# A gated GNN followed by a GCN on one core: the adjacency turned by VectorE in 4-byte words, and the last TensorE transposes of activations replaced by exchanges

## The chip, the core and the metric

The kernel runs on one core of a Trainium2 chip. Five engines take their instructions from queues of their own: TensorE (PE, with its weight loads shown apart as PEld), VectorE (DVE), ScalarE (ACT), GpSimd (POOL), and SyncE (SP), which here only issues DMA transfers. The metric is the device time in microseconds (us) of one execution. A measured time is the median of several runs; the profile is of one more execution, with its own time.

## The reference, cut to what matters

Sixteen graphs of 1024 nodes with 128 features each; `adj` is a 0/1 matrix of 1024 x 1024 for every graph.

```
h = relu(layernorm(x))
for i in range(4):                          # gated GNN, every graph by itself
    hw = h @ weight[i]
    m  = adj^T @ hw                         # einsum 'bjn,bjd->bnd'
    r  = sigmoid(m @ w_ih.T + h @ w_hh.T ...);  z = sigmoid(...)
    n  = tanh(...);  h = (1 - z) * n + z * h
x = x + h * nodemask
h = relu(layernorm(x))
for i in range(4):                          # GCN
    h = relu(adj @ (h @ W[i]) + b[i])       # einsum 'bnm,bmc->bnc'
    h = gamma[i] * (h - mean) * rsqrt(var + 1e-5) + beta[i]   # mean, var over all graphs and nodes
x = x + h
```

The first network multiplies by the transposed adjacency, which is what a plain load of rows gives to TensorE as moving operand. The second multiplies by the adjacency itself, so the matrix must be turned once for each graph.

## The kernel before

**Two stages.** `exact_path` first runs the gated network over all graphs, and then the GCN layer by layer over all graphs. Between them lie, in DRAM, the turned adjacency in bf16 (`adjT_d`), the sum after the first network (`xmid_d`) and its normalised form (`ymid_d`). A flag (`low`) notes whether the adjacency was exact in bf16; a general path, not run with these inputs, would follow otherwise.

**The gated stage** works on two streams, `sa` (graphs 0, 2, 4 ...) and `sb` (1, 3, 5 ...). A half step (`half_step(one, two)`) does the gates of a layer for stream `two` and, behind it on TensorE, the aggregation of the next layer for stream `one`; then the roles change. Eight half steps take each stream through four layers. On TensorE a half step is 24 gate matmuls (two passes each, L1008) in two halves of 512 nodes and 32 aggregation matmuls (L526: 8 blocks of 128 rows, a high and a low part of the features, two halves of nodes). The features are split in a rounded high part and a remainder (`high`, `low`, L933 and L940) so that TensorE's faster number format loses nothing.

On VectorE a half of a half step is, in the order of its queue: the reset gate (L1027, L1028), `less` (L1044, or L1042 for a stream's first layer), `scaled` (L1048), `low` of the other stream (L940 or L956), `mixed` (L1052), and a transposition of the new features in 32 x 32 blocks (L728). The 32 x 32 blocks are put in their places through DRAM: SP writes them (`exchange_out`, L599) and reads them back in four pieces (`exchange_in`, L606). So most of the turns between features-by-nodes and nodes-by-features need no TensorE.

An order written by hand (`tc.manual_schedule`) fixes all queues in this stage. Other work is entered in an agenda (`at(clock, place, work)`) and taken out at named places of a half step: "start" and "load" before the gates, "beside0/1" within them, "mid" between the halves (GpSimd first waits there for the first half's result, the `pace` copy of L1114), "gap" after both halves. After a graph's last layer, `plan` enters the sum with x and its statistics (`tail_sums`, "gap" two half steps later), the store of that sum, the normalisation, and then the load and statistics of the stream's next graph (`next_sums`, "gap" five half steps later).

**Turning the adjacency.** GpSimd rounds each 128-row block to bf16 (`transpose_rows`, L623), SP issues a DMA transpose of it (L624), and after eight blocks GpSimd issues a store of 2 MB (L637). The generator `transposes` and the class `Feed` spread these over the half steps. There are two bf16 buffers, so a cast waits until an earlier DMA transpose has read its buffer. GpSimd also rounds the loaded rows for the aggregation (L579).

**TensorE transposes that are left** (matmuls by the identity): 8 for x of graph 1 (`turn(sb.y, ...)`, L708; 8 more for graph 0 stay), 8 for the first new features of graph 0 (`split_step`, which is `features_times` with `w is None`, L499), 16 for the last features of graphs 14 and 15 (`last_tail`, L743), and 8 in each of three GCN layers for graph 0 (`raw_split`, L499).

**The GCN stage** is placed by a scheduler. For each graph SP loads eight bf16 blocks of the turned adjacency (L1347), VectorE and ScalarE widen them to the matmul format into 12 row buffers (L1352, L1350), TensorE does 32 aggregation matmuls. In layer 0 `first_split` loads `ymid_d` (into one of four shared buffers) and splits it. In later layers `conv_input` normalises the features of a graph on ScalarE (L1384). The even graphs' blocks use the buffer of tag "adjT" (one), the odd graphs' the eight of tag "half".

**The end.** The last statistics, the normalisation of all 16 graphs (L1548 in halves for graphs 0 and 1, L1542 whole for the others), 128 TensorE transposes (L1554), the sum with x (L1556) and 33 output transfers by SP (L1557).

Of the kernel before, what the change touches and what calls it, by code (L numbers as in the profile page):

```python
# [11 lines left out]
U16 = mybir.dt.uint16  # L12
# [329 lines left out]
def exact_path(  # L342
# [149 lines left out]
    def features_times(w, hT, hw, g, name):  # L492

        pt = tmp(f"hw_{name}_{g}")
        for q in range(BH):
            j = g * BH + q
            src = hT[:, j * P : (j + 1) * P]
            if w is None:
                nc.tensor.transpose(pt[:, q * P : (q + 1) * P], src, ident)  # L499
            else:  # L500
                nc.tensor.matmul(pt[:, q * P : (q + 1) * P], src, w, start=True, stop=True)
        cols = slice(g * HALF, (g + 1) * HALF)
        nc.scalar.copy(hw[0][:, cols], pt)  # L503
        nc.vector.tensor_sub(hw[1][:, cols], pt, hw[0][:, cols].bitcast(F32))
# [30 lines left out]
    with ExitStack() as st:  # L535
# [35 lines left out]

        def stage_rows(b, stage, js):
            for j in js:
                nc.sync.dma_start(stage[j % 4], adj[b][j * P : (j + 1) * P, :])
# [7 lines left out]
        def glance(b, stage, js):  # L582

            junk = work.tile([P, N], BF16, tag="junk", name=f"junk{b}_{js[0]}", bufs=1)
# [5 lines left out]
        def row_sums(rows, js):  # L590

            for j in js:
                junk = work.tile([P, N], BF16, tag="junk", name=f"summed{j}", bufs=1)
                nc.scalar.activation(junk, rows[j].bitcast(F32), AF.Copy, accum_out=by_row[:, j : j + 1])

        def exchange_out(t, name, d=None):
            if d is None:
                d = rawd.tile([P, HALF], F32, tag="cross", name=f"cross_{name}", bufs=8)
            nc.sync.dma_start(d, t)  # L599
# [8 lines left out]
        def pair_in(d, t):  # L608

            src = d.rearrange("h (t r) (s x) -> s r (h t) x", t=4, s=4)  # L610
            for s in range(4):
                nc.sync.dma_start(t[s * 32 : (s + 1) * 32, :].rearrange("r (a x) -> r a x", a=8), src[s])
# [7 lines left out]
        def transpose_rows(b, row, j, adjT):  # L620

            t = work.tile([P, N], BF16, tag="half1", name=f"half{b}_{j}", bufs=2)
            nc.gpsimd.tensor_copy(t, row.bitcast(F32))  # L623
            return lambda: nc.sync.dma_start_transpose(adjT[:, :, j * P : (j + 1) * P], t)  # L624

        def transposes(batches):

            for b, rows in batches:
                adjT = turned_tile(f"adjT{b}")
                ahead = transpose_rows(b, rows[0], 0, adjT)  # L630
                for j in range(NB):
                    go = ahead
                    if j + 1 < NB:
                        ahead = transpose_rows(b, rows[j + 1], j + 1, adjT)
                    go()
                    yield j
                nc.gpsimd.dma_start(adjT_d[b].rearrange("k p n -> p k n"), adjT)  # L637
                yield NB

        class Feed:  # L640


            jobs, full, stored = iter(()), False, False

            def some(self, n):
                for _ in range(n):
                    if not self.full:
                        self.full = next(self.jobs, None) == NB - 1

            def store(self):  # L650
                if self.full and not self.stored:
                    self.stored = next(self.jobs) == NB

            def next_step(self):
                if self.stored:
                    self.full = self.stored = False

        feed, agenda = Feed(), {}
# [68 lines left out]
        def half_out(t, src, hf, name, d=None):  # L727
            turned = nc.vector.transpose(by_nodes(t), four_ways(src[:, hf * HALF : (hf + 1) * HALF]))  # L728
            return exchange_out(t, f"{name}_{hf}", d), turned
# [4 lines left out]
        def tail_sums(b, xt, hT, parts=None):  # L734

            for hf in range(NH):
                if parts:
                    pt = by_nodes(parts[hf])
                else:
                    pt = tmp(f"pt_x{b}_{hf}")  # L740
                    for q in range(BH):
                        k = hf * BH + q
                        nc.tensor.transpose(pt[:, q * P : (q + 1) * P], hT[:, k * P : (k + 1) * P], ident)  # L743
                    pt = four_ways(pt)
                for q in range(BH):
                    k = hf * BH + q
                    xk = xt[:, k, :].rearrange("p (a c) -> p a c", a=4)
                    mask = maskT[:, b * NB + k : b * NB + k + 1]
                    nc.vector.scalar_tensor_tensor(xk, pt[:, q, :, :], mask, xk, ALU.mult, ALU.add)
            return norm_stats(xt, f"mid{b}")  # L750
# [13 lines left out]

        def last_tail(b, xt, hT):
            nt = tail_sums(b, xt, hT)
            y = y_mid(b) if b + 1 < B else xt.rearrange("p k c -> p (k c)")
            store_xmid(b, xt)

            def rest():  # L770
                norm_apply(xt, y, nt)
                store_ymid(b, y)

            return rest
# [3 lines left out]
        class Stream:  # L778
# [54 lines left out]
            def plan(self, n, tail=None):  # L833

                if tail:
                    b, xt, hT, parts = tail
                    end = {}

                    def sums():
                        end["norm"] = tail_sums(b, xt, hT, parts)  # L840
# [11 lines left out]
                    at(n + 5, "mid", lambda: store_ymid(b, end["y"]))  # L852
                if self.b + 2 < B:
# [5 lines left out]
                    at(n + 7, "end", self.ins_away)  # L859

# [44 lines left out]
            def half_away(self, hf):  # L905

                if self.i + 1 - hf == L and self.b + 2 < B:
                    if hf == 0:
                        self.pair = rawd.tile([NH, P, HALF], F32, tag="pair", name=f"pair_out{self.b}", bufs=4)
                    half_out(cross_tile(f"t_out{self.b}_{hf}"), self.new, hf, f"out{self.b}", self.pair[hf])  # L910
# [5 lines left out]
            def halves_back(self):  # L916
                nm = f"{self.b}_{self.i}"
                self.backs = [cross_tile(f"n_h{nm}_{hf}") for hf in range(NH)]
# [25 lines left out]
            def split_step(self):  # L944
                nm = f"{self.b}_{self.i}"
                self.hw = hw_tiles(self.b, f"ghw{nm}")
                for g in range(NH):
                    features_times(None, self.hT, self.hw, g, f"g{nm}")

# [11 lines left out]
            def agg_rows(self, js):  # L961
# [3 lines left out]
                if js[-1] == NB - 1:  # L965
                    self.m = []
                    for hf in range(NH):
                        m = work.tile([P, HALF], F32, tag="m", name=f"m{self.b}_{self.i}_{hf}", bufs=4)
# [22 lines left out]
            def products(self, hf):  # L991
# [28 lines left out]
                self.z = work.tile([P, HALF], F32, tag="z", name=f"z{nm}")  # L1020
# [36 lines left out]
            def finish(self):  # L1057
# [3 lines left out]
                args = self.b, self.xt, self.hT  # L1061
                self.b, self.i = self.b + 2, 0
                if self.b >= B:
                    self.rest = last_tail(*args)
# [3 lines left out]
                parts = [args[-1][:, hf * HALF : (hf + 1) * HALF] for hf in range(NH)]  # L1068

                last = args[-1]  # L1070
                at(clock[0] + 1, "ins", lambda: pair_in(ins, h_in))
                at(clock[0] + 1, "outs", lambda: pair_in(outs, last))
                self.plan(clock[0], (*args, parts))
# [10 lines left out]
        def first_step(one, two, gated, halfway, rest=None):  # L1084

            if one.outs:
                one.halves_back()
                feed.jobs = transposes([(s.b, s.rows) for s in (sa, sb)])
            else:
                one.split_step()  # L1090
            feed.some(2)
            two.gate_step(0)
            two.half_away(0)
            if one.outs:
                for g in range(NH):
                    one.high(g)
                    one.low(g)
            feed.some(2)
            two.gate_step(1)
            two.half_away(1)  # L1100
            gated()
            one.agg_step(0)
# [507 lines left out]
```

## Time and profile before

| what | value |
|---|---|
| median of 3 runs | 1767.48 us (1766.98 to 1768.0) |
| profiled execution, its time | 1767.31 us |
| span of its instructions | 1765.3 us |
| granted TensorE clock, mean | 0.998 |
| DMA, mean over the span | 228 GB/s |
| ACT ended by waits for VectorE's reset gate (L1031) | 151.9 us idle |
| GpSimd idle in front of the bf16 casts (L623), for DMA transposes | 402.7 us |

The span runs from the first to the last instruction; about 2 us of the execution lie around it. In the tables of the profile a group gives the line, the engine, the operation, the tile written and read, the shapes, the count, then the time in which at least one of the group was busy, the mean of one in ns, and the idle time of the engine just ahead of them. In the timeline a row has start, length, engine, line, operation, tiles and, in brackets, the idle time before it with what ended it. Matmuls overlap, so the time per matmul is read from the starts, not from the length of one.

### The profile page before, as it was taken

Reading aid. Unit: us, or ns where it says so; the run is one execution under the profiler, and the core shown is the slowest. Engines: PE = TensorE matmul, PEld = TensorE weight load, DVE = VectorE, ACT = ScalarE, POOL = GpSimd, SP = SyncE. Lnnn points to the kernel's source line nnn. Section 1 sums busy time; section 2 is a strip of 40 time slices with the busy share of each in tenths; the row PEclk is TensorE's granted clock in tenths of the full one; section 3 lists DMA queues with packets and bytes.
Section 4 is the critical chain, followed back from the end, with each engine's and each line's share of the span. In section 5 each row is a group of like instructions: output and inputs, shape, how many; then the busy total and the mean of one; then the engine's idle time right before and its main releaser. Section 6 shows DMA issues by size and latency. Waiting matters only on the chain. (4 is left out here: it accounts for less than half of the span.)

```text
span 1765.3 us, 22293 instructions
## 1 busy us (share of the span) xinstructions
PE 1747.9 (99%) x6710; PEld 1189.1 (67%) x6710; DVE 1289.1 (73%) x2311; ACT 1123.1 (64%) x1729; POOL 374.3 (21%) x404
## 2 busy tenths in 40 slices
PE   9999999999999999999999999999999999999997
PEld 5565656565656565656565656577778888888886
DVE  7686977877877877877787686776666666666665
ACT  5366556557566556655755654486777777767765
POOL 4124323322322332422422323110100000000010
PEclk9999999999999999999999999999999999999999
DMA  7479788677777777778867968888865766757666
GB/s 256 97 195 301 153 217 296 163 208 249 205 200 235 222 188 229 248 183 216 274 158 192 307 150 223 283 310 304 300 219 198 252 224 221 255 202 264 216 235 256
DMA packets 377778, 401.74 MB, mean 228 GB/s; under 512 B 158396, under 2 KB 255456, under 8 KB 377648
## 3 DMA queue, kind: packets, MB, share of 16 engines
q1 hardware_dynamic: 358736, 331.98, 62.9%
q0 software_dynamic: 18384, 67.99, 11.1%
q8 instruction: 55, 0.90, 0.2%
q14 instruction: 75, 0.61, 0.1%
q10 hardware_dynamic: 528, 0.26, 0.0%
HBM read 268.52 MB, written 98.05 MB: 208 GB/s over the span
## 5 line engine op out<-in xcount | busy, mean ns | idle before, releaser
L526 PE MATMUL pm<-row,ghw 128*128 128x512 f32 x2048 | 504.4, 403 | 0.6 <-POOL row L565 0.5
L526 PEld LDWEIGHTS pm<-row,ghw 128*128 128x128 f32 x2048 | 383.6, 188 | 107.7 <-issue 25.5
L526 PE MATMUL pc_m<-wide,chw 128*128 128x512 f32 x1024 | 245.2, 395 | 0.0
L623 POOL CAST half<-row 128x1024 bf16<-128x1024 f32 x128 | 148.6, 1171 | 421.3 <-DMA adjT<-half 402.7
L526 PEld LDWEIGHTS pc_m<-wide,chw 128*128 128x128 f32 x1024 | 190.4, 188 | 41.9 <-issue 3.8
L1031 ACT ACTIVATE r<-r,vecs 128x512 f32<-128x512 f32 x128 | 92.3, 721 | 153.6 <-DVE r L1028 151.9
L526 PE MATMUL pc_g_r<-wide,chw 128*128 128x512 f32 x464 | 186.9, 403 | 0.3 <-ACT chw L503 0.3
L969 ACT COPY m<-pm 128x512 f32<-128x512 f32 x128 | 68.7, 588 | 185.0 <-PE pm L526 185.0
L526 PE MATMUL pc_g_z<-wide,chw 128*128 128x512 f32 x464 | 181.0, 390 | 0.0
L1027 DVE SCALAR_TENSOR_TENSOR r<-g_hn,vecs,r 128x512 f32<-128x512 f32 x128 | 93.2, 728 | 119.4 <-ACT r L1026 68.4
L579 POOL CAST row<-stage 128x1024 fp32r<-128x1024 f32 x112 | 129.1, 1160 | 214.1 <-DMA stage<-in_adj_dram 177.0
L1352 DVE CAST wide<-block 128x1024 fp32r<-128x1024 bf16 x160 | 109.5, 691 | 74.1 <-PE pc_m L526 49.2
L1352 DVE CAST wide<-packed 128x1024 fp32r<-128x1024 bf16 x160 | 110.2, 693 | 70.9 <-PE pc_g_z L526 53.2
L1350 ACT CAST wide<-packed 128x1024 fp32r<-128x1024 bf16 x96 | 100.6, 1047 | 56.4 <-PE pc_m L526 27.6
L1350 ACT CAST wide<-block 128x1024 fp32r<-128x1024 bf16 x96 | 100.4, 1049 | 53.5 <-PE pc_g_z L526 27.7
L1008 PE MATMUL g_r<-m,w_mT 128*128 128x512 f32 x256 | 130.8, 592 | 0.2 <-ACT m L969 0.2
L1008 PE MATMUL g_z<-m,w_mT 128*128 128x512 f32 x256 | 130.7, 592 | 0.0
L1008 PE MATMUL g_xn<-m,w_mT 128*128 128x512 f32 x256 | 130.7, 592 | 0.0
L1048 DVE TENSOR_TENSOR h<-h,z 128x512 f32<-128x512 f32 x128 | 112.6, 880 | 14.4 <-ACT z L1035 2.2
L1026 ACT ACTIVATE r<-g_r,brz 128x512 f32<-128x512 f32 x128 | 87.9, 687 | 48.0 <-PE g_r L1008 47.6
L1400 DVE BATCH_NORM_STATS2 stats<-feat 128x6 f32<-128x512 f32 x128 | 84.1, 685 | 46.6 <-ACT feat L1399 45.6
L1044 DVE TENSOR_TENSOR h<-h,r 128x512 f32<-128x512 f32 x96 | 73.4, 765 | 56.4 <-ACT r L1031 56.4
(186 smaller groups left out, 2817.1 us busy)
## 6 DMA issues: line engine op xcount, KB each, us to landing
block<-adjT_d SPq DMA_DIRECT2D x256, 256.0 KB, 4.7
packed<-adjT_d SPq DMA_DIRECT2D x256, 256.0 KB, 5.7
stage<-in_adj_dram SPq DMA_DIRECT2D x120, 512.0 KB, 5.4
adjT_d<-adjT POOLq DMA_DIRECT2D x16, 2048.0 KB, 8.4
cross_h<-t_h SPq DMA_DIRECT2D x94, 256.0 KB, 2.5
n_h<-cross_h SPq DMA_DIRECT2D x376, 64.0 KB, 2.1
xmid_d<-x POOLq DMA_DIRECT2D x16, 512.0 KB, 7.2
y<-ymid_d POOLq DMA_DIRECT2D x16, 512.0 KB, 6.8
```

The source lines that it names most:

```text
L526: nc.tensor.matmul(pm[hf], hw[s][:, j * P : (j + 1) * P], rows[j][:, hf * HALF : (hf + 1) * HALF], start=(j == 0 and s == 0), stop=(j == N ...
L579: nc.gpsimd.tensor_copy(t, stage[j % 4])
L623: nc.gpsimd.tensor_copy(t, row.bitcast(F32))
L1008: nc.tensor.matmul(po, wT[:, i, g * C : (g + 1) * C], rhs, start=start, stop=stop)
L1026: nc.scalar.activation(r, pr, AF.Sigmoid, bias=brz[:, 3 * i : 3 * i + 1])
L1027: nc.vector.scalar_tensor_tensor(r, phn, b_hn(i), r, ALU.add, ALU.mult)
L1031: nc.scalar.activation(self.r, self.r, AF.Tanh, bias=b_in(self.i))
L1044: nc.vector.tensor_sub(ho, hin, self.r)
L1048: nc.vector.tensor_mul(ho, ho, self.z)
L1350: nc.scalar.copy(r, t)
L1352: nc.vector.tensor_copy(r, t)
L1400: nc.vector.bn_stats(stats[:, b * NH + hf, :], dst)
```

## The change

The adjacency: for each pair of row blocks j and j + 4 GpSimd writes the two bf16 roundings interleaved, so that two 16-bit values form a 4-byte word; VectorE transposes 32 x 32 blocks of words into `adjT`; SP stores the result in four transfers that put the blocks in place. `Feed`, `transposes` and `transpose_rows` go. The nodes of the turned matrix then lie in pairs, so the GCN reads its features through rearranged views (`in_pairs`, `in_order`), and in two halves. The remaining activations are exchanged through DRAM, too: x and h of the first step, h of the last layer of graphs 14 and 15 (whose sums and normalisation move into layer 0 of the GCN, `chores`), and graph 0's features in each GCN layer (`raw_turned`). Looks at the first rows' low bits move from VectorE to ScalarE (`first_glance`). `ymid_d` of graphs 2 to 15 is loaded straight into `feat`. The last `conv_done` works its second half in two parts.

```diff
@@ turning the adjacency
-        def transpose_rows(b, row, j, adjT):
-            t = work.tile([P, N], BF16, tag="half1", name=f"half{b}_{j}", bufs=2)
-            nc.gpsimd.tensor_copy(t, row.bitcast(F32))
-            return lambda: nc.sync.dma_start_transpose(adjT[:, :, j * P : (j + 1) * P], t)
...
+        def pair_rows(b, rows, j):
+            w = work.tile([P, 2 * N], BF16, tag="pair", name=f"pair{b}_{j}", bufs=3)
+            halves = w.rearrange("p (n o) -> p n o", o=2)
+            for o in range(2):
+                nc.gpsimd.tensor_copy(halves[:, :, o], rows[4 * o + j].bitcast(F32))
+            return w
+
+        def turn_pair(w, adjT, j):
+            words = adjT.rearrange("p k n -> p (k n)").bitcast(F32).rearrange("p (b j i) -> p j b i", j=4, i=32)
+            nc.vector.transpose(words[:, j], w.bitcast(F32).rearrange("p (b c) -> p b c", c=32))
+
+        def store_turned(b, adjT, eng):
+            src = adjT.rearrange("p k n -> p (k n)").rearrange("p (b x) -> p b x", x=N // 4)
+            dst = adjT_d[b].rearrange("k (a c) (s x) -> s c (k a) x", a=4, s=4)
+            for k in range(4):
+                eng.dma_start(dst[k], src[k * 32 : (k + 1) * 32])
@@ plan(self, n, tail)
+                if self is sa:
+                    at(n + 4, "start", lambda: pairs(range(3)))
+                    at(n + 4, "gap", lambda: turns(range(1)))
+                    at(n + 4, "gap", lambda: pairs(range(3, 4)))
+                    at(n + 4, "gap", lambda: turns(range(1, 4)))
...
+                if self is sa:
+                    at(n + 5, "load", lambda: store_turned(self.b, room[0], nc.sync))
+                else:
+                    at(n + 4, "mid", lambda: pairs(range(2)))
+                    at(n + 4, "gap", lambda: turns(range(2)))
+                    at(n + 5, "start", lambda: pairs(range(2, 4)))
+                    at(n + 5, "gap", lambda: turns(range(2, 4)))
+                    at(n + 6, "load", lambda: store_turned(self.b, room[0], nc.sync))
@@ half_away(self, hf)
-                if self.i + 1 - hf == L and self.b + 2 < B:
+                if self.i + 1 - hf == L:
+                    end = self.b + 2 >= B
...
+                    eng = nc.gpsimd if end else nc.sync
@@ half_step
-            feed.some(counts[0])
...
@@ first step: x of graph 1 and h of graph 0
-            sb.agg_rows(range(4))
-            turn(sb.y, "in1", h1)
...
+            in0 = turned_half(sb.y, h1, 0, "in1")
+            exchange_in(in0, half_of(h1, 0))
...
+            out1 = turned_half(sa.new, sa.y, 1, "h0_1")
+            exchange_in(out1, half_of(sa.y, 1))
@@ GCN
+    def scaled_nodes(eng, hT, b, aff, n0, n):
+        to, src = in_order(hT[:, n0 : n0 + n]), in_pairs(feat[b], n0, n)
...
+            nc.scalar.activation(to, src, AF.Identity, bias=aff[1], scale=aff[0])
...
-    def conv_input(b, i, aff, parts=1):
+    def conv_input(b, i, aff):
         hT = work.tile([P, N], F32, tag="h", name=f"bn{b}_{i}", bufs=3)
+        for hf in range(NH):
+            scaled_nodes(nc.scalar, hT, b, aff, hf * HALF, HALF)
...
-        yt = flat(f"y{b}").rearrange("p k c -> p (k c)")
+        yt = flat(f"y{b}").rearrange("p k c -> p (k c)") if b < 2 else feat[b]
...
+    def raw_turned(i):
+        d = dram.tile([NH, P, HALF], F32, tag=f"raw{i}", name=f"raw_d{i}")
+        blocks = feat[0].rearrange("c (x i o) -> c x o i", i=32, o=2)
+        for hf in range(NH):
...
+            nc.vector.transpose(
+                t.rearrange("p (x o c) -> p x o c", o=2, c=32), blocks[:, hf * 8 : (hf + 1) * 8]
+            )
+            nc.gpsimd.dma_start(d[hf], t)
...
     def raw_split(i):
...
-            features_times(None, feat[0], hw, g, f"c0_{i}")
+            nc.scalar.copy(hi, backs[:, g])
+            nc.vector.tensor_sub(lo, backs[:, g], hi.bitcast(F32))
...
+    def chores(s, b):
...
+        return [
+            lambda: pair_in(s.pair, parts, nc.gpsimd),
+            lambda: sums(0),
+            last_sums,
+            lambda: blocks(0),
+            last_blocks,
+        ]
+    late = dict(zip(range(2, 7), chores(sa, B - 2)))
+    late.update(zip(range(7, 12), chores(sb, B - 1)))
@@ the end
-        if b > 1:
-            nc.scalar.activation(hT, feat[b], AF.Identity, bias=aff[1], scale=aff[0])
         for n0, n in pieces(b):
...
+            scaled_nodes(nc.vector if b == 0 and n0 == 0 else nc.scalar, hT, b, aff, n0, n)
```

## The prediction

> **What bounds the kernel now.** I read the page's busy shares first, then the slices, then a table of three stretches, then the timeline of one step.
>
> ```profile
> PE 1747.9 (99%) x6710; PEld 1189.1 (67%) x6710; DVE 1289.1 (73%) x2311; ACT 1123.1 (64%) x1729; POOL 374.3 (21%) x404
> ...
> PE   9999999999999999999999999999999999999997
> ...
> PEclk9999999999999999999999999999999999999999
> ```
>
> ```profile
> 300.00:500.00 200.00, 200.00 (x641) 120.65 (x640) 161.53 (x308) 121.29 (x210) 64.45 (x65) 1.00 0.75 209
> 1200.00:1400.00 200.00, 199.66 (x934) 159.82 (x933) 130.25 (x193) 145.49 (x184) 8.52 (x14) 1.00 0.73 252
> 1600.00:1765.00 165.00, 153.60 (x836) 131.72 (x835) 104.37 (x169) 108.63 (x130) 11.34 (x19) 0.98 0.67 237
> ```
>
> TensorE is busy throughout, at a full clock; in the table (stretch, length, busy PE, PEld, DVE, ACT, POOL, clock, DMA share, GB/s) it is idle only at the very end. It loses 17.4 us of 1765.3 (1765.3 - 1747.9), some 4.9 at the start and 11.4 at the end. So time falls only as TensorE's work falls, and rises as soon as something makes TensorE wait. The second number to keep is DVE's 161.53 of 200 in the gated stage: 81%, against 65% in the GCN stage.
>
> ```profile
> 302.32 7.83 PE L526 MATMUL pm<-row,ghw 128*128 128x512 f32 x32
> ...
> 319.89 7.83 PE L526 MATMUL pm<-row,ghw 128*128 128x512 f32 x32
> ```
>
> From one aggregation to the next is 17.57 us, and that repeats in every half step but the first few: TensorE's own pace. Two early ones are longer by 0.66 and 0.78 us.
>
> **TensorE's part: -6.1 us.** These groups go (8 of the 16 of L708, the others wholly): 24 + 16 + 8 + 8 = 56 transposes.
>
> ```profile
> L499 PE MATMUL hw_c<-ident,feat 128*128 128x128 f32 x24 | 3.1, 272 | 0.0
> L743 PE MATMUL pt_x<-ident,h 128*128 128x128 f32 x16 | 2.3, 274 | 0.1
> L708 PE MATMUL pt_in<-ident,y_in 128*128 128x128 f32 x16 | 2.1, 272 | 0.0
> L499 PE MATMUL hw_g<-ident,h 128*128 128x128 f32 x8 | 1.0, 272 | 0.0
> ```
>
> The means are latencies. By starts, eight of them hold TensorE from 39.34 to 40.21 us, and eight in the GCN from 1135.93 to 1136.80: 0.109 us each, 56 x 0.109 = 6.1. No matmul is added. The wait of 0.65 us in front of the gates at 46.17 (DVE's split of graph 0's new features) goes; ScalarE's copies of m, which the new order puts behind another copy (0.48 us), are late next, about 0.45 us: -0.2 net. In the two early long half steps DVE loses looks at low bits to ScalarE: I take half of their 1.44 us, -0.7 (0 to -1.4).
>
> **VectorE's part in the gated stage.** Added: 64 turns of 128 x 1024 words, 4 for each graph.
>
> ```profile
> L728 DVE STREAM_TRANSPOSE t_h<-h 128x512 f32<-128x512 f32 x94 | 66.9, 712 | 3.3
> L1411 DVE TENSOR_TENSOR chw<-y,chw 128x1024 fp32r<-128x1024 f32 x16 | 19.6, 1222 | 2.1 <-ACT chw L1410 2.1
> L1048 DVE TENSOR_TENSOR h<-h,z 128x512 f32<-128x512 f32 x128 | 112.6, 880 | 14.4 <-ACT z L1035 2.2
> ```
>
> No row has a word transpose 1024 wide. Twice the 512-wide row is 1.42; other DVE work grows from 0.69 to 1.22 us when its width doubles, so I take 1.24 (1.22 to 1.42): 80 us in all. A rule prices it otherwise: the Trainium skill, page "VectorE: DVE Perf Modes", section "The three transpose paths", has 311 ns for one 128 x 128 block on VectorE. A turn is eight blocks of words, by that an estimate of 2.5 us. The row has four 4-byte blocks in 712 ns, 178 each, and decides. By the row `sa` puts 4 x 1.24 = 5.0 us into one gap of eight half steps and `sb` 2.5 into each of two; by the rule it would be 10 and 5, and the gap would overrun by far.
>
> Does it fit? DVE is busy for 11 to 13 us of the 17.57 in the half steps that take `sa`'s turns, so 5.0 more nearly fills them; those with `sb`'s turns have 13 to 15 and get 2.5. What counts is when `low` of the first half ends, since the aggregation's third matmul (0.49 us in) needs it. In most half steps it ends 1.5 to 2.5 us ahead of the aggregation, but behind the tail sums (L749) only -0.02 to 1.30 us ahead, in four of seven cases under 0.7. Counted along DVE's queue with the new work in it: where `sa`'s turns are, `low` still ends some 0.25 us ahead; where a gap holds statistics (3.15 us) and `sb`'s turns (2.5), the next reset gate starts 3.2 us late, 2.0 to 2.4 of it in time that DVE idles there today, and with 4.41 us from reset gate to `low` this ends 0.57 us behind the aggregation's start, against the 0.49 allowed. These sums are good to some tenths. So I take 0.1 to 0.5, 0.3 us in the middle, for the eight half steps of `sb`'s kind and nothing for `sa`'s: +2.4 us (0 to 20, the upper end if all fifteen lag by 1.3 us).
>
> **GpSimd's part.** The 128 casts stay (strided 2-byte output now), but their DMA transposes go, and with them the waits that spread them out:
>
> ```profile
> L623 POOL CAST half<-row 128x1024 bf16<-128x1024 f32 x128 | 148.6, 1171 | 421.3 <-DMA adjT<-half 402.7
> ```
>
> An idle POOL cost nothing by itself, but six casts will now run back to back. What a cast does to DVE is in this row of the timeline:
>
> ```profile
> 342.51 3.74 DVE L749 SCALAR_TENSOR_TENSOR x<-h,maskT,x 128x128 f32<-128x128 f32 x8
> ...
> 358.96 3.07 DVE L1048 TENSOR_TENSOR h<-h,z 128x512 f32<-128x512 f32 x1
> ...
> 359.45 2.03 POOL L623 CAST half<-row 128x1024 bf16<-128x1024 f32 x2
> ```
>
> L1048, with two SBUF inputs, takes 0.69 us alone and here 3.07, until both casts have ended; its mean is 0.88. In the whole trace 113 DVE operations are slowed, by 84.8 us. The Trainium skill, page "SBUF — State Buffer", section "Who interferes with whom", says why: the pair of ports that the two engines share is locked for a whole instruction, and a DVE instruction with two SBUF inputs blocks against GpSimd's reads. It speaks against this change. By that rule one operation waits for one cast (at most 1.04), and then has its turn; at 40 of 43 seams between two casts with DVE waiting, DVE did get in. At the other three it waited through. If that were the case in a run of six, one operation would wait 6 x 1.04 = 6.2 us, and TensorE some 4. I take the 40 of 43; cast time 1.04 to 1.17 as before, since input and count are the same (up to 2.1, if a strided 2-byte output halved the rate, which no row shows).
>
> **SP's and DMA's part: 0.** 128 transposes of 3.9 us median and 16 stores of 2 MB on POOL's queue leave; 64 stores of 512 KB on SP's queue come, issued at "load", ahead of the gates' exchanges. They wait for the last turn, and behind them in SP's order stand the stage loads and `exchange_in`. As the turns are in the gap before, the wait is over then. If they were still late, the exchange behind them would be, and each us of it would reach the reset gates: 0 to 0.5 us a graph, 8 in all. The bytes stored stay the same 32 MB, and DMA is at 0.75 of its share.
>
> **The entry of the GCN: +1.3 us (0 to 5).** `y` of graph 2 now goes into `feat`, issued by POOL only behind `sb`'s last work, about 1151.9 us on the old axis.
>
> ```profile
> y<-ymid_d POOLq DMA_DIRECT2D x16, 512.0 KB, 6.8
> ```
>
> It lands 6.8 us later; then ScalarE's high part and DVE's low part (1.22 us) stand in the queues ahead of rows that graph 1's aggregation needs. Counted along, its fifth row comes 1.3 us late.
>
> **The rest.** `conv_input` in halves: 2 x 0.705 in place of 1.133 us on ScalarE, +0.3 a graph, beside TensorE (ScalarE is at 145.49 of 200). The exchange of graph 0's features in each layer hides behind the aggregation of the previous graph, as DVE's rows lead TensorE by up to 12, 11.7 us; uncovered it would be a DMA store and load, 2.1 and 2.5 us, three times. Half of `conv_done` in two parts: -0.2.
>
> The tail: ScalarE normalises 14 graphs in 14 x 1.133 = 15.9 us before, in 28 x 0.705 = 19.7 after, and becomes slower than TensorE's 112 transposes at 0.1425 us (16.0). But this stage ends with its outputs:
>
> ```profile
> out_dram<-xo SPq DMA_DIRECT2D x7, 256.0 KB, 2.1
> out_dram<-xo_h SPq DMA_DIRECT2D x8, 256.0 KB, 4.3
> ```
>
> Latency grows from 2.1 to 4.3 us since 256 KB land only every 0.69 to 0.80 us; a supply at 0.705 is about that pace. I take 0 (-1 to +3.3).
>
> **Sum** against the profiled execution, 1767.31: -6.1 - 0.2 - 0.7 + 2.4 + 1.3 - 0.2 = -3.5, so 1763.8. The median, 1767.48, is 0.2 higher: 1764.0.
>
> **Rivals.** A difference under 0.2%, 3.5 us, is about what a measurement here can't tell from no change; so "faster" is below 1763.95 and my point lies on the edge of it.
> *A, the forecast*, 1758 to 1767: TensorE's work drops out, small stalls take part of it. For it: the exact 17.57 us. Chance 0.46, some 0.37 of it below the edge.
> *B, given back*: the ledger's margins of some tenths are wrong by half a us on DVE, so 15 half steps lose 0.4 each (6 us in place of 2.4): 1767.6. For it: margins of 0.02 to 0.5 us in four of seven half steps. Against: DVE is idle elsewhere and can catch up. Chance 0.15.
> *C, slower*: runs of six casts hold DVE's two-input operations (or a strided cast is slower than 1.17). From the point where the delay exceeds some 0.5 us in the half steps with `sa`'s turns and 2.3 in `sb`'s, each us goes to TensorE: 1 us in 15 half steps is 15 in place of the 2.4 counted, 1764.0 - 2.4 + 15 = 1776.6. For it: the 3.07 row. Against: 40 of 43. Chance 0.30.
> *D, the tail is bound by ScalarE*: +3.3, so 1767.3. For it: 19.7 against 16.0. Against: output latencies. Chance 0.09.
> That DVE's turn doesn't do what it says is no rival: words are moved whole. B and D mostly fall within 0.2%, C above. With shares of each on both sides: faster 0.43, same 0.26, slower 0.31. The range, 1757.5 (no stall at all, relief and tail at their better ends: 1764.0 - 2.4 - 1.3 - 0.7 - 1 = 1758.6, and 1 for the size of a transpose) to 1780 (C), leaves out 2 in 10, mostly above.
>
> **What would show it.** Right: TensorE's count down by 56 and no group of identity transposes but L708's eight; half steps still 17.57 us; DVE at 78% (1289 + 80 of 1762); turns at 1.24 us; idle before aggregations below 0.5 us. Wrong: half steps over 18 us in the two kinds with turns, `low` as their releaser, a mean of the `scaled` row (L1048) well over 880 ns (C); POOL casts above 1.2 us; PE waiting for `wide` in graph 1 of layer 0 by more than 5 us; ScalarE's `bn` as the end's releaser with idle PE (D). A turn of 2.5 us would upset the whole ledger.

## The result, and the profile after

| | before | after |
|---|---|---|
| median | 1767.43 us (1766.98 to 1768.0, 4 runs) | 1845.8 us (1844.88 to 1849.49, 4 runs) |
| ratio, with its 95% interval | | 1.0447 [1.0429, 1.0465] |
| span of the profiled execution | 1765.3 us | 1844.2 us |
| mean granted TensorE clock | 0.998 | 0.984 |

The change costs 78 us, where 3.5 us of gain were forecast. The first row of the page after and three groups of the table of lines (busy time, mean ns of one, idle time ahead with what ended it):

```profile
PE 1775.8 (96%) x6654; PEld 1200.0 (65%) x6654; DVE 1396.8 (76%) x2378; ACT 1145.7 (62%) x1804; POOL 389.2 (21%) x412
...
L523 PE MATMUL pm<-row,ghw 128*128 128x512 f32 x2048 | 526.7, 414 | 46.8 <-DVE ghw L942 44.1
...
L633 POOL CAST pair<-row 128x1024 bf16<-128x1024 f32 x128 | 163.0, 1344 | 136.0 <-DVE adjT L639 112.5
...
L942 DVE TENSOR_TENSOR ghw<-n_h,ghw 128x512 fp32r<-128x512 f32 x94 | 156.9, 1670 | 0.2 <-ACT ghw L935 0.2
```

TensorE has its 56 instructions less (6710 - 6654), and yet is busy for 27.9 us more and idle for 51 us more. The aggregation, which waited 0.6 us in all, now waits 46.8, and 44.1 of them for one operation: `low` of the first half (L942), the subtraction that makes the remainder of the features. Both its inputs lie in SBUF. Before, it had this row:

```profile
L940 DVE TENSOR_TENSOR ghw<-n_h,ghw 128x512 fp32r<-128x512 f32 x94 | 71.7, 763 | 18.1 <-ACT ghw L933 18.1
```

Same shape, same count, 763 against 1670 ns. The timeline of one half step after the change (start, length, engine, line, operation, tiles) says when:

```profile
346.91 0.91 POOL L743 DMA_DIRECT2D xmid_d<-x  x1
...
347.82 7.55 POOL L633 CAST pair<-row 128x1024 bf16<-128x1024 f32 x6
...
348.55 4.66 PE L523 MATMUL pm<-row,ghw 128*128 128x512 f32 x18
348.70 7.17 DVE L942 TENSOR_TENSOR ghw<-n_h,ghw 128x512 fp32r<-128x512 f32 x1
...
355.93 4.99 PE L523 MATMUL pm<-row,ghw 128*128 128x512 f32 x14 [2.72 <-DVE ghw L942]
```

GpSimd issues a store, then does six casts of the adjacency without a pause. The subtraction begins 0.88 us into the first cast and ends at 355.87, 0.5 us behind the last: it waited through all six. TensorE runs out of matmuls that need only the high part, and stands still for 2.72 us. That is not all it loses. The table of two stretches (stretch, length, busy PE, PEld, DVE, ACT, POOL, granted clock, DMA share, GB/s):

```profile
348.50:355.00 6.50, 4.70 (x20) 3.38 (x18) 6.50 (x2) 2.88 (x4) 6.50 (x6) 1.00 0.37 112
355.00:360.00 5.00, 4.07 (x11) 3.27 (x12) 4.79 (x12) 0.00 (x0) 0.37 (x1) 0.66 0.08 29
```

After the pause the mean clock of 5 us is 0.66 (0.50 from 356 to 359). So this half step takes 22.11 us in place of 17.57: 2.72 idle, about 1.8 by the clock. Fourteen half steps have this wait, and lose 65 us together; nearly all between are at 17.57. Ten of the fourteen (22.1 to 22.9 us, and one of 27.5) have the lower clock as well; the other four (20.4 to 20.7) have a pause of about the same length, 2.5 to 2.8 us, and keep the full clock. The second half step of all has the wait too, behind an issue of the GCN's weights.

One run of six casts in the same execution has no issue right ahead of it, only the `pace` copy, and there the subtraction got in:

```profile
89.65 0.19 POOL L1080 COPY pace<-h 128x1 f32<-128x1 f32 x1 [10.11 <-DVE h L1048]
89.78 8.04 POOL L633 CAST pair<-row 128x1024 bf16<-128x1024 f32 x6
...
91.68 1.16 DVE L942 TENSOR_TENSOR ghw<-n_h,ghw 128x512 fp32r<-128x512 f32 x1
```

By stages, from the starts of TensorE's matmuls in the timeline (the first GCN aggregation, the first of the second layer, the first output transpose, the end):

| us | before | after | difference |
|---|---|---|---|
| to the first GCN aggregation | 1147.5 | 1214.4 | +67.0 |
| first GCN layer | 144.7 | 156.6 | +11.9 |
| three further layers | 443.3 | 441.2 | -2.0 |
| last stage | 29.9 | 32.0 | +2.1 |

The first two lines got experiments of their own. In the first GCN layer TensorE waits for a copy of ScalarE (L1433; the first row of the table of waits is the gated stage's), and the DMA engines are full:

```profile
PE pm L523 <- DVE ghw L942: 44.1, 15, 6.6
PE pw_g_hn L1434 <- ACT cm L1433: 6.0, 2, 4.1
```

(us in total, times, longest), and

```profile
1214.40:1290.00 75.60, 67.90 (x253) 49.11 (x252) 49.29 (x112) 48.58 (x72) 23.22 (x37) 0.93 1.00 339
```

against the same stretch of that layer before, with a share of 0.88 and a full clock:

```profile
1147.50:1223.00 75.50, 75.35 (x309) 57.04 (x308) 53.67 (x97) 61.36 (x87) 9.69 (x14) 1.00 0.88 312
```

### The profile page after: what moved, and what is told of

Read it like the earlier page. It is cut to its first block, busy times and chain, and to the rows that moved or that the text cites. A ratio compares the mean times of both kernels' runs of the same rounds, so it can differ in the third digit from the quotient of the medians.

```text
span 1844.2 us, 22093 instructions
## 1 busy us (share of the span) xinstructions
PE 1775.8 (96%) x6654; PEld 1200.0 (65%) x6654; DVE 1396.8 (76%) x2378; ACT 1145.7 (62%) x1804; POOL 389.2 (21%) x412
## 5 line engine op out<-in xcount | busy, mean ns | idle before, releaser
L523 PE MATMUL pm<-row,ghw 128*128 128x512 f32 x2048 | 526.7, 414 | 46.8 <-DVE ghw L942 44.1
L523 PEld LDWEIGHTS pm<-row,ghw 128*128 128x128 f32 x2048 | 395.8, 194 | 163.6 <-DVE ghw L942 50.5
L633 POOL CAST pair<-row 128x1024 bf16<-128x1024 f32 x128 | 163.0, 1344 | 136.0 <-DVE adjT L639 112.5
L1027 ACT ACTIVATE r<-r,vecs 128x512 f32<-128x512 f32 x128 | 92.2, 720 | 143.9 <-DVE r L1024 142.4
L942 DVE TENSOR_TENSOR ghw<-n_h,ghw 128x512 fp32r<-128x512 f32 x94 | 156.9, 1670 | 0.2 <-ACT ghw L935 0.2
L1413 DVE BATCH_NORM_STATS2 stats<-feat 128x6 f32<-128x512 f32 x129 | 83.5, 681 | 44.1 <-ACT feat L1412 43.4
```

The source lines that it names most:

```text
L523: nc.tensor.matmul(pm[hf], hw[s][:, j * P : (j + 1) * P], rows[j][:, hf * HALF : (hf + 1) * HALF], start=(j == 0 and s == 0), stop=(j == N ...
L633: nc.gpsimd.tensor_copy(halves[:, :, o], rows[4 * o + j].bitcast(F32))
L942: nc.vector.tensor_sub(lo, back, hi.bitcast(F32))
L1027: nc.scalar.activation(self.r, self.r, AF.Tanh, bias=b_in(self.i))
L1413: nc.vector.bn_stats(stats[:, b * NH + hf + k, :], dst)
```

## The experiments

Three theories stood at first. F: the strided output of the new casts keeps VectorE out. Q: any run of casts without a wait does. D: a DMA issued by GpSimd right ahead of the run does. A time without an interval is that of one execution, to be compared with 1845.8 us; the kernel before took 1765.8 to 1768.7 beside them. The stages of a run are read from its trace like those of the table.

### The form of the casts

```diff
-                nc.gpsimd.tensor_copy(halves[:, :, o], rows[4 * o + j].bitcast(F32))
+                nc.gpsimd.tensor_copy(w[:, o * N : (o + 1) * N], rows[4 * o + j].bitcast(F32))
```

> The rounded rows are written side by side instead of interleaved, so the turned adjacency and with it the GCN's output are other numbers; instructions and their order are those of the changed kernel. All theories: the low part of the features (the DVE subtraction that stalls) is what costs the time. Theory F (the strided 2-byte output is what keeps VectorE out): its mean falls from 1670 ns to below 900, time 1762 to 1775. Theory Q (a run of casts that wait for nothing keeps it out, whatever the form) and theory D (a DMA issue on GpSimd's queue right ahead of the run does): casts take 0.98 us in place of 1.25, a wait of 5.9 us remains in place of 7.1, mean 1.4 to 1.55 us, time 1820 to 1840.

1805.65 us. This kernel leaves out the interleaving, so its output is another; its instructions and their order stay. The casts follow each other every 0.98 us (1.25 in the changed kernel), and the subtraction still ends just behind the last of six, in most cases after 5.5 to 5.6 us; its mean is 1427 ns. F falls as the cause of the wait; the form sets only the length of the run. The time is below what Q and D had: most of these half steps lose 1.5 us and not 4.5, since TensorE's pause is shorter and the clock stays full behind it. The same 14 matmuls that took 4.99 us above:

```profile
347.40 3.48 PE L523 MATMUL pm<-row,ghw 128*128 128x512 f32 x14 [1.16 <-DVE ghw L941]
```

### The issue ahead of the casts

```diff
-            nc.gpsimd.dma_start(xmid_d[b].rearrange("(k p) c -> p k c", p=P), xt)
+            nc.sync.dma_start(xmid_d[b].rearrange("(k p) c -> p k c", p=P), xt)
-            nc.gpsimd.dma_start(ymid_d[b], y)
+            nc.sync.dma_start(ymid_d[b], y)
```

> The stores of the sum after the gated network and of its normalised form are issued by SP in place of GpSimd, so that no DMA issue stands ahead of a run of six casts. Theory D: the subtraction gets in after one or two casts, mean below 1000 ns, time 1765 to 1785. Theories F and Q: still the whole run, mean above 1500 ns, time 1838 to 1850 (the run starts 0.5 to 0.9 us earlier, so it may hit another operation of the same kind, with the same length of wait).

1794.37 us, mean 794 ns. The same place of the timeline, now without a store ahead:

```profile
340.00 0.19 POOL L1080 COPY pace<-h 128x1 f32<-128x1 f32 x1 [18.83 <-DVE h L1048]
340.13 9.35 POOL L633 CAST pair<-row 128x1024 bf16<-128x1024 f32 x6
...
342.03 1.17 DVE L942 TENSOR_TENSOR ghw<-n_h,ghw 128x512 fp32r<-128x512 f32 x1
...
343.12 1.77 DVE L1038 TENSOR_TENSOR h<-h_in,r 128x512 f32<-128x512 f32 x1
...
345.00 1.59 DVE L1044 TENSOR_TENSOR h<-h,z 128x512 f32<-128x512 f32 x1
```

The same six casts take 9.35 us in place of 7.55, and VectorE's operations with two SBUF inputs run between them, about one for each cast. From the 12th half step to the GCN nearly all are at 17.57 us, the rest below 18.3 but for one of 20.63. D holds. Q falls: here a run of casts without a wait in it lets VectorE in. The total is 9 us above D's upper end for two reasons of other places: on SP the last two graphs' stores stand ahead of the adjacency loads (first GCN layer 162.6 us in place of 156.6), and two half steps near the end (18.19 and 20.63 us) wait for the flag (below).

### A small operation in the seam

```diff
                 nc.gpsimd.tensor_copy(halves[:, :, o], rows[4 * o + j].bitcast(F32))
+                nc.gpsimd.tensor_copy(tiny, eps_t)
```

> A copy of one column (128 x 1) follows each of the 128 casts on GpSimd, without a wait. Theory Q, if any instruction boundary of another kind opens the seam: mean of the subtraction below 1000 ns, time 1765 to 1785. Theories F and D, and Q if only a real wait opens it: the run is 6 x 0.1 to 0.2 us longer, mean 1.7 to 1.9 us, time 1846 to 1860.

1855.42 us, mean 1783 ns: a boundary to another operation, without a wait, does not let VectorE in.

### Four bytes

To the run with the stores on SP comes one tiny transfer, in the even graphs' half steps alone:

```diff
+            def tiny_out(self):
+                nc.gpsimd.dma_start(tiny_d, eps_t[:1, :])
...
+                    at(n + 4, "start", self.tiny_out)
                     at(n + 4, "start", lambda: pairs(range(3)))
```

> The run with the stores on SP, with one more transfer of 4 bytes to DRAM issued by GpSimd just ahead of the casts of the even graphs (stream sa), and none ahead of those of the odd ones. Theory D1: the size doesn't matter, the subtraction behind each of these seven or eight issues waits for the whole run again, 7.1 us, in half steps of the sa kind only (about 22 us against 17.57), total 1794 + 7 x 4.6 = 1822 to 1832. Rival D2 (the transfer's time holds it): the wait is 1 to 3 us, half steps at most 18.5, total 1794 to 1802.

1817.07 us, 22.7 more than without it. An even graph's half step, and then an odd one's:

```profile
342.70 0.55 POOL L807 DMA_DIRECT2D tiny_d<-eps_t  x1 [0.31 <-issue]
...
343.24 7.56 POOL L634 CAST pair<-row 128x1024 bf16<-128x1024 f32 x6
...
344.07 4.66 PE L524 MATMUL pm<-row,ghw 128*128 128x512 f32 x18
344.22 7.08 DVE L947 TENSOR_TENSOR ghw<-n_h,ghw 128x512 fp32r<-128x512 f32 x1
```

```profile
381.20 9.37 POOL L634 CAST pair<-row 128x1024 bf16<-128x1024 f32 x6
...
383.11 1.18 DVE L947 TENSOR_TENSOR ghw<-n_h,ghw 128x512 fp32r<-128x512 f32 x1
```

7.08 us with an issue of four bytes ahead, 1.18 without one, in the same execution. It is the issue, not the store's size; nor its time on the way, for the four bytes land in 1.7 us (median). Each of the seven half steps loses 3.3 us (22.8 / 7), less than the 4.6 expected: five of them (20.2 to 20.6 us) keep the full clock, though the pause is nearly as long as above.

```profile
351.36 3.48 PE L524 MATMUL pm<-row,ghw 128*128 128x512 f32 x14 [2.63 <-DVE ghw L947]
```

### The issue, then a wait, then the casts

```diff
-                    at(n + 3, "mid", lambda: store_xmid(b, xt))
+                    at(n + 3, "pre", lambda: store_xmid(b, xt))
...
-            if (clock[0], "mid") in agenda:
+            early = (clock[0], "pre") in agenda
+            due("pre")
+            if early or (clock[0], "mid") in agenda:
                 mids(two)
```

and the same for the store of y. The stores are issued ahead of the `pace` copy, which waits.

> The two stores stay on GpSimd but are issued ahead of its wait for the first half's result and no longer between that wait and the casts. Theory D1 (the issue leaves GpSimd holding the port until its queue next has to wait): the wait ends it, the subtraction's mean falls to 0.75 to 0.85 us, the half steps are 17.57 to 17.9 us, total 1790 to 1800, like the run with the stores on SP. Rival D2 (a store on its way, some 4.5 us to landing, is what holds it): the wait comes within that time in some half steps, so part of the subtractions still take 3 to 7 us, total 1805 to 1840.

1783.82 us, mean 785 ns, half steps at 17.57 with 17.8 to 18.1 in every eighth; the two that wait for the flag are at 18.19 and 20.64 again. With a wait of GpSimd between issue and casts VectorE gets in, with the stores still on GpSimd's queue (D1). It is 62 us for two stores issued earlier.

For these stores the issue also lies over 5 us ahead of the casts, so it could be the time and not the wait that ends the matter. One place tells them apart, with another issue that has a wait of only 2.3 us behind it:

```profile
1079.78 0.55 POOL L1507 DMA_DIRECT2D w_hhT<-xmid_d  x1 [3.33 <-PE g_r L1004]
1082.63 0.19 POOL L1080 COPY pace<-h 128x1 f32<-128x1 f32 x1 [2.30 <-DVE h L1048]
1082.75 9.35 POOL L633 CAST pair<-row 128x1024 bf16<-128x1024 f32 x6
...
1084.65 1.19 DVE L942 TENSOR_TENSOR ghw<-n_h,ghw 128x512 fp32r<-128x512 f32 x1
```

The subtraction gets in 4.3 us behind the issue's end, where in the changed kernel one was held until 8.0 us behind it. Nor is it the `pace` copy as such: in the run with 128 x 1 copies, which do not wait, VectorE did not get in.

### The casts on ScalarE

```diff
-                nc.gpsimd.tensor_copy(halves[:, :, o], rows[4 * o + j].bitcast(F32))
+                nc.scalar.copy(halves[:, :, o], rows[4 * o + j].bitcast(F32))
```

> The 128 casts go to ScalarE at the same places of the schedule; GpSimd has none of them. If the port shared by VectorE and GpSimd is the whole of the loss: the subtraction's mean falls below 850 ns, TensorE's clock is back at 0.998, time 1762 to 1772. Rival: VectorE's added 75 us of turns is a loss of its own, then some 1775 to 1790 with stalls in the half steps with turns and no long subtraction. ScalarE's own lag (six casts of about 1.1 us ahead of the gates' sigmoids) can hide the answer: then TensorE waits for ScalarE's results at the same half steps, up to 1840.

1875.84 us. The subtraction is at 718 ns, so GpSimd's casts were its trouble; but VectorE now waits for ScalarE's sigmoid, in half steps of 24.5 to 26.2 us for the even graphs and mostly 21.9 for the odd ones:

```profile
DVE r L1023 <- ACT r L1022: 167.1, 46, 8.4
```

The last clause of the expectation had this, with too small a price (1840); ScalarE's lag hides what the turns of VectorE cost, so this run leaves that open.

### The loads of y

```diff
-        yt = flat(f"y{b}").rearrange("p k c -> p (k c)") if b < 2 else feat[b]
+        yt = flat(f"y{b}").rearrange("p k c -> p (k c)")
```

> The changed kernel, with the normalised features of graphs 2 to 15 loaded into the four shared buffers again (as before the change) and not straight into each graph's own; nothing else differs. From the first GCN aggregation to the first of its second layer the kernel before takes 144.7 us, the changed one 156.6. Theory B (loads that wait for no buffer are issued in a burst, seven of 512 KB in some 8 us, and delay the adjacency rows): 144.5 to 147, at most one such load per 9 us, total 1832 to 1838. Rival K (the last two graphs' sums and normalisation, moved into this layer, are what delays ScalarE and the rows): 154 to 158, total 1843 to 1849.

1837.91 us; the first GCN layer takes 148.1 us in place of 156.6. In the changed kernel GpSimd sends the loads off at once, and the adjacency rows come late:

```profile
1219.52 1.16 POOL L1420 DMA_DIRECT2D feat<-ymid_d  x2
...
1223.01 1.11 POOL L1420 DMA_DIRECT2D feat<-ymid_d  x2
1224.47 0.53 POOL L1420 DMA_DIRECT2D feat<-ymid_d  x1 [0.35 <-DMA feat<-ymid_d]
1225.95 0.53 POOL L1420 DMA_DIRECT2D feat<-ymid_d  x1 [0.95 <-DMA feat<-ymid_d]
```

```profile
1231.46 1.04 ACT L1347 CAST wide<-packed 128x1024 fp32r<-128x1024 bf16 x1 [4.77 <-DMA packed<-adjT_d]
```

Six loads of 512 KB in 7 us, then ScalarE idle for 4.77 us for a row of the adjacency. With four buffers each load waits until an older one has been used, one in about 9 us. Theory B holds for 8.5 of the 11.9 us (156.6 - 148.1); the layer is still 1.1 us above B's range, so something else is in it.

### All cures, and what is left of the first layer

The next run has the stores on SP, the shared buffers for y, and three small edits: the weights' load for the GCN on SP (it stood ahead of four casts in the second half step), the flag's VectorE operations queued behind the last gate (one waited 3.86 us for TensorE, ahead of a `low`), and GpSimd scales one half in four in the last stage.

```diff
-            nc.gpsimd.dma_start(w_c, c_w.rearrange("l c d -> c l d"))
+            nc.sync.dma_start(w_c, c_w.rearrange("l c d -> c l d"))
...
+    with tc.issue_after(sb.last_dve.ins):
...
+        nc.vector.tensor_copy(flag_i, pt[:1, :1])
...
-            scaled_nodes(nc.vector if b == 0 and n0 == 0 else nc.scalar, hT, b, aff, n0, n)
+            eng = nc.vector if b == 0 and n0 == 0 else nc.gpsimd if b > 1 and b % 2 and n0 else nc.scalar
+            scaled_nodes(eng, hT, b, aff, n0, n)
```

> Both cures and three small ones together: stores on SP; the y loads in shared buffers; the load of the GCN weights on SP (it was issued on GpSimd ahead of four casts); the flag's operations on VectorE queued behind the last gate; in the last stage GpSimd scales one half of four. If the ledger of the changed kernel (gated stage +67, of which all but about 0.5 in two half steps per 16 goes; entry layer +11.9; last stage +2.1) is complete: span 1759 to 1764, time 1761 to 1766, below the kernel before by 2 to 7 us. Rival: VectorE's 75 us of turns cost something by themselves that the long waits hid: then half steps with turns stay above 18 us and the time is 1768 to 1780.

1778.27 us, a miss: it lies in the rival's range, but not for the rival's reason. The gated stage ends at 1146.6 us, 0.9 ahead of before, and its half steps are at 17.9 us or below, so VectorE's 75 us of turns cost TensorE no more than 0.3 us in every eighth half step. It is the first layer, with the stores on SP, that takes 156.4 us. The next run has them on GpSimd ahead of the wait:

> All cures together, now with the stores on GpSimd's queue ahead of its wait (on SP they stood ahead of the adjacency loads in the GCN's first layer, which took 156.4 us in the last combination): shared buffers for y, the weights' load on SP, the flag queued last, GpSimd with one half of four in the last stage. By stages: start of the GCN at 1146.6 us (before 1147.5), first layer 146 to 148.5 (before 144.7), further layers 2.1 less than before, last stage 30.0 to 30.5 (29.9). Total 1765 to 1768, within 0.2% of before. If the ledger is wrong and the changed kernel's turns or exchanges have a price not seen yet, 1770 to 1778.

1770.42 us, ratio 1.0016 [1.0008, 1.0024]. To the GCN 1145.9 us, first layer 151.9, further layers 442.0, last stage 30.4. The total and the first layer are again above the forecast (1768 and 148.5 at most). What is left over the kernel before is in the first layer (+7.2) and the last stage (+0.5).

Then the end of graphs 14 and 15 was moved by one graph:

```diff
-    late = dict(zip(range(2, 7), chores(sa, B - 2)))
-    late.update(zip(range(7, 12), chores(sb, B - 1)))
+    late = dict(zip(range(3, 8), chores(sa, B - 2)))
+    late.update(zip(range(8, 13), chores(sb, B - 1)))
```

> The same, with the last two graphs' sums, normalisation and stores put one graph later in the first GCN layer (graphs 3 to 12 in place of 2 to 11). If the first layer's remaining 1.5 to 3.5 us over the kernel before come from these transfers falling into the stretch in which the DMA engines are full (97 to 104% in the changed kernel's first 90 us, 1183 to 1201 only in the kernel before): first layer 144.5 to 146, total 1762 to 1766. If it is the work on ScalarE and VectorE, no difference of more than 0.5 us to the run beside it.

1776.11 us, ratio 1.0045 [1.0031, 1.0058], first layer 153.4, 1.5 longer than in the run beside it, which neither branch had: a shift by one graph does not help. Its gated stage is 3.2 us longer too, though nothing is changed there; that stays unexplained.

The last cause was tried by taking it away: `last_tail` of the kernel before, with its 16 transposes, in place of `chores`.

```diff
-                if self.i + 1 - hf == L:
+                if self.i + 1 - hf == L and self.b + 2 < B:
...
+                    self.rest = last_tail(*args, last)
...
+            with tc.issue_after(sb.last_act.ins):
+                sa.rest()
+            sb.finish()
...
-    late.update(zip(range(7, 12), chores(sb, B - 1)))
+    late = {}
...
+                with tc.issue_after(last.ins):
+                    sb.rest()
```

> The cured version, with the end of graphs 14 and 15 as it was before the change: 16 TensorE transposes (1.7 us), sums and normalisation at the end of the gated stage, nothing of them in the first GCN layer. Theory K (these exchanges, sums and stores in the first layer are what it is long by: 151.9 us in the cured version, 144.7 before): first layer 144.5 to 146, total 1770.4 - 6.5 + 1.7 = 1764 to 1767. Rival M (something else of the first layer, graph 0's exchange of features or the loads, makes it long): 150 to 152, total 1770 to 1772.

1766.67 us, ratio 0.9994 [0.9986, 1.0002]; first layer 143.9 us. Theory K holds for the cured version: what was moved into the first layer costs it 8.0 us (151.9 - 143.9), and takes 2.4 off the gated stage (1148.3 - 1145.9), the 16 transposes' 1.7 among them. Whether it is its transfers or its work on ScalarE and VectorE stays open. TensorE is back at its bound, also in a stretch of this layer in which the DMA engines are full, so a full share by itself does not make it wait:

```profile
PE 1744.7 (99%) x6670; PEld 1184.0 (67%) x6670; DVE 1351.2 (77%) x2374; ACT 1141.1 (65%) x1799; POOL 413.2 (23%) x406
...
1184.00:1224.00 40.00, 40.00 (x162) 30.14 (x161) 27.14 (x38) 28.33 (x38) 3.15 (x5) 1.00 1.02 368
```

Last, on top of this, the odd graphs' last four casts are put behind GpSimd's next wait:

```diff
-                    at(n + 5, "start", lambda: pairs(range(2, 4)))
+                    at(n + 5, "mid", lambda: pairs(range(2, 4)))
```

> The same, with the second pair of casts of an odd graph moved half a step on (behind GpSimd's next wait), so that four casts and not six follow each other there. In the cured version seven half steps, those with six casts for an odd graph, take 17.8 to 18.1 us in place of 17.57. If four operations of VectorE that each wait for a cast are what is late there: these half steps return to 17.57, 1.5 to 2 us less than the run beside it, total 1762 to 1765. If VectorE's own turns make it late, no difference above 0.5 us.

1771.64 us, ratio 1.0022 [1.0014, 1.003], 5 more than the run beside it, where 1.5 to 2 less or no difference was expected. The half steps in question return to 17.57, but the ones after them, with the moved casts, take 18.1 in most cases, and others lose too. Six casts in a row, once VectorE can get in, are not worth spreading in this way.

No version was measurably better than the kernel before; that with the old tail is equal to it.

## Why the prediction was wrong

**The step that failed** is in GpSimd's part: "I take the 40 of 43". The 43 seams were counted as one population, and the three in which VectorE waited through both casts were taken as chance. All three were in runs that began right behind a DMA issue of GpSimd; ahead of the shown one of 358.96 stand

```profile
357.69 0.89 POOL L637 DMA_DIRECT2D adjT_d<-adjT  x1 [2.24 <-DMA adjT<-half]
358.57 0.89 POOL L760 DMA_DIRECT2D xmid_d<-x  x1
```

The change leaves the two stores of each graph on GpSimd's queue and puts the casts right behind them; fourteen of the sixteen graphs get such a run of six. So the sum has no term for this, and fourteen half steps lose 65 us. By the rule that the prediction cites, a lock lasts for one instruction; here VectorE stayed out for all the casts that followed the issue without a wait. Sorted by what stands ahead of the run, the trace of before had the sign of it: seven pairs of casts stand right behind an issue there, all three misses are among these seven, and none is among the others.

**Rival C** had much of the mechanism, but not the issue, and even the length: "6 x 1.04 = 6.2 us" for the operation, "TensorE some 4"; measured 7.1 us, and 4.7 a half step in the mean (65.2 / 14). What was mis-sized is the term "1 us in 15 half steps": it priced a milder form than its own sentence described. Priced by that sentence it is 15 x 4 = 60, near to the 67 of the gated stage, but in part by luck: TensorE's pause itself is 2.7 us in most of them, and no step had its clock, which adds about 1.8 in ten of the fourteen. Of its signs, `low` as the releaser came; the `scaled` row, put at well over 880 ns, fell to 755 (now L1044), for it was `low` that met the casts.

**The entry of the GCN**, "+1.3 us (0 to 5)", measured +11.9. The one late load that was counted is not what decides. Missed were the loads that lose their wait, 8.5 us, and `chores`, costed at nothing without a reason and worth 8.0 us in the cured version. The two do not add up to 11.9: the run with the shared buffers alone, which has `chores` too, is at 148.1, and the cured one at 151.9. Where these 3.8 us come from, no run shows.

**Right:** TensorE's transposes (56 fewer; the further layers, with two of their three groups of eight, are 2.0 us shorter, 1.3 in the cured versions, where 0.109 each makes 1.7); a turn of 1.24 us, measured 1213 ns:

```profile
L639 DVE STREAM_TRANSPOSE adjT<-pair 128x1024 f32<-128x1024 f32 x64 | 75.2, 1213 | 3.8 <-POOL pair L633 3.6
```

and the stalls by VectorE's fuller queue, "0.1 to 0.5, 0.3 us in the middle" for the odd graphs and nothing for the even ones: with the long wait gone these half steps take 17.8 to 18.1 and 17.57 us. The estimate of 2.5 us a turn, weighed beside the 1.24, was double; the row cited for it is for bf16 blocks, and a word has twice the bytes. The casts were put a little low, at 1.04 to 1.17 us a piece against 1.25. **The tail**, 0 (-1 to +3.3), is +2.1 in the changed kernel, as rival D said: a half takes ScalarE some 854 ns, not the 705 of the sum,

```profile
L1389 ACT ACTIVATE bn<-feat,bn_sh,bn_sc 128x512 f32<-128x512 f32 (+1 forms) x32 | 24.5, 854 | 0.7 <-DVE bn_sc L1374 0.7
```

24.5 us of ScalarE in the last stage, where before 14 whole ones and 4 pieces took 18.7 (16.0 + 2.7); TensorE's weight loads waited 6.7 us for it, before 0.9. No run changes this alone.

## What to carry to other kernels

When one engine can hold another up, sort the few bad cases in the trace by what came just ahead of them before calling them chance; here a DMA issue in the same queue made a wait for one cast into a wait for six. A wait that is taken away was also a pace: the buffers that held loads back kept DMA free for the rows that TensorE needed. And cost each part of a change in the stage in which it lands: even with the long waits gone, a gain of 6 us spread over three stages was outweighed by the work moved into the GCN's first layer.

## What the runs showed of the hardware

A DMA issue on GpSimd (0.5 to 0.9 us, of 4 bytes or 512 KB) followed without a wait by six casts shut out VectorE's subtraction, which has two SBUF inputs, for 6.8 to 8.0 us, until the last cast: 14 of 14 times in the changed kernel. In the runs without such an issue, or with a wait of GpSimd between, the same operation took at most 1.6 us. A 128 x 1 copy in the seams did not end it. In the trace of before, seven pairs of casts stand right behind an issue. Where the first two-input operation to run into the casts began ahead of the last issue or at most 0.2 us into it, it got in (four pairs); where it began 0.35 us or more behind the issue's start, it did not (three). Why, no run shows.

Ten of the fourteen pauses of TensorE (2.7 to 3.4 us, one of 6.7) were followed by a clock of 0.50, for 3.4 us in nine of them; four pauses of 2.5 to 2.8 us were not, nor were those of 1.2 to 1.5 us in the run with dense casts. What decides between pauses of the same length, no run shows.
